# Layer 1 of a four-layer graph network: the later neighbours' numbers of blocks 4 to 7 made at step 12 instead of step 4, and in another PSUM bank

## The chip, the cores and the metric

The kernel runs on one core of a Trainium2 chip. A core has five engines that run side by side, each through its own list of instructions and in order: TensorE (PE; its weight loads are listed as PEld), VectorE (DVE), ScalarE (ACT), GpSimd (POOL) and SyncE (SP), which only starts transfers. They wait for one another by semaphores. TensorE writes into PSUM, which has eight banks of 512 float32 columns on each of 128 partitions; VectorE and ScalarE read it from there.

The metric is the time of one execution on the device, in microseconds (us). 0.2% of it is 1.15 us.

## The reference

Four layers pass over one graph of 4096 nodes with 64 features and an adjacency matrix of 4096 x 4096 zeros and ones (about four neighbours in a row). Each layer takes `h = max(layernorm(x), 0)` and adds something to `x`. Layer 0 is an attention with masked sigmoid scores, layers 2 and 3 are plain sums over neighbours. The change lies in layer 1:

```python
support = input @ weight
mask = (adj != 0).astype(support.dtype)
rank = jnp.cumsum(mask, axis=1)
deg = rank[:, -1:]
k = jnp.minimum(deg, float(MAX_NEIGH))          # MAX_NEIGH = 100
pos = rank - (deg - k)
w = mask * jnp.where(pos > 0, DECAY ** (k - pos), 0.0)   # DECAY = 0.5
out = w @ support + bias
```

A neighbour's weight is thus 0.5 to the power of the number of neighbours of the same row that come after it.

## The kernel before

**Tiles.** The adjacency matrix is kept transposed in on-chip memory as zeros and ones in fp8, in eight tiles `mask0` to `mask7`. A tile, or block `ib`, holds 512 rows of the matrix (`IB`); in it lie 32 chunks `t` of 128 neighbours each (`NT`), a chunk on 128 partitions. Blocks 0 to 3 are quad 0, blocks 4 to 7 quad 1.

**How a weight is made.** For a chunk, one matmul (`cnt`, L1500 in `counted`) counts for every neighbour the later ones, scaled so that the result, written as a 16-bit integer, is the bit pattern of 0.5 to that power in bf16. The constant matrix `after` counts the later ones inside the chunk. The number of neighbours in later chunks must be known beforehand; it is brought in through the last two partitions of the chunk, 126 and 127 (`KEPT`, `LANES`), where such numbers stand in the place of the mask's own rows. These two rows of the mask were copied aside earlier into `apart_m` (`taken`), are handled as a 33rd unit of their block (`t = -1`), and are put back afterwards (`given_back`, L1453).

**The numbers.** `chunks_counted(quad)` counts the neighbours of every chunk of a quad into a PSUM bank and copies the counts to `many`. `numbered(quad)` sums them over the later chunks: one matmul with `beyond` and four small ones with `pair` into a bank `pn`. VectorE then writes two fp8 rows `two`, the number capped at 120 and what is left of it, and copies started on SyncE's queue put them into partitions 126 and 127 of the quad's four masks, eight copies for quad 1. `numbered(0)` runs while the chunks of quad 1 are counted. `numbered(1)` runs inside the loop of layer 1.

**The loop of layer 1.** The blocks are taken in pairs (`GROUPS`: 0 and 1, 2 and 3, 4 and 5, 6 and 7). A pair has 66 units, its chunks from the last to the first and then the two rows set apart, and a step `k` (counted from 1) takes four of them: four `cnt` matmuls; four weights `w`, each a pass from PSUM to a 16-bit tile on ScalarE or VectorE; and the four products (`acc`, L1535) of the step before. So the pair 0, 1 takes steps 1 to 17, and quad 1 is first read at the beginning of the third pair, at 375.31 us of the profile. After the counts of each step, `step()` lets other work go on by one piece: the end of layer 0 for the last rows (`rows0`), the degrees (`degrees_of`), the rows of a finished pair (`rows1`). Then `check(2)` may run: VectorE checks that a piece of the adjacency matrix, read again from memory in float32 (`ckw`, 512 KB, three buffers, loads on SyncE's queue at L438), holds zeros and ones. A check first issues the next load, which waits until its buffer is read, and then checks the oldest one.

**The order** is written out by hand (`manual_schedule`); each engine runs its instructions as the program names them. Which engine makes a `w` is decided when the program is built: `Planned` sums what each engine was given, and VectorE takes a `w` where ScalarE would be late by the plan. All VectorE and ScalarE instructions go through a helper and are shown at L73.

**Banks.** The counts go round five banks, `COUNTS = (0, 1, 2, 5, 6)`, by a running index `turns[0]`; a step needs four of them. Two more banks hold the sums of the pair's blocks. The eighth, tag `pr` of pool `pm`, is the one in which rows are turned: `degrees_of` (`pd`), `rows0`, and from the second pair on `rows1` (`pr`, L1322) use it. Before the change `pn` takes the next of the five counting banks for both quads.

**SyncE's queue** carries, in the program's order: the loads for the checks, the copies of `two`, the two copies of `features_apart` (`apart_s`, L1485: the features that belong to the rows set apart, issued once the last rows of layer 0 are split on VectorE into `s2a`, read at step 17's products), and the copies of `given_back`.

Of the kernel before, what the change touches and what calls it, by code (L numbers as in the profile page):

```python
# [11 lines left out]
F32 = mybir.dt.float32  # L12
# [14 lines left out]
P = 128  # L27
NT = N // P
IB = 512
# [49 lines left out]
def kernel(  # L79
# [87 lines left out]
    def model(general):  # L167

        sfx = "_g" if general else ""
# [5 lines left out]
        def pool(name, bufs, on=stack, **kw):  # L175
            return on.enter_context(tc.tile_pool(name=name + sfx, bufs=bufs, **kw))
# [49 lines left out]
        pm = pool("pm", 1, space=PSUM)  # L226
# [143 lines left out]
        def push(job, lag):  # L370

            jobs.append([job, lag])
# [37 lines left out]
        def lane_of(ib, n):  # L410

            return masks[ib][KEPT + n : KEPT + n + 1, :, :]
# [780 lines left out]
        with tc.manual_schedule():  # L1193
# [20 lines left out]
            k, done = NG + 2, NG  # L1214
# [58 lines left out]
        def bank(b, name, shape=(P, IB)):  # L1273
            on = first_bank if b == COUNTS[-1] else banks
            return on.tile(list(shape), F32, tag=f"bank{b}", name=name + sfx)


        COUNTS = (0, 1, 2, 5, 6)
# [169 lines left out]
        many, turns = {}, [0]  # L1448
# [5 lines left out]

        def numbered(quad):

            pn = bank(COUNTS[turns[0] % len(COUNTS)], f"pn_{quad}")
            turns[0] += 1
            nc.tensor.matmul(
                pn, beyond, many[quad], start=True, stop=False, skip_group_check=True  # L1460
            )
            for q in range(QUAD):
                nc.tensor.matmul(
                    pn[q * NT : (q + 1) * NT, :], pair[:, quad, :], apart_m[:, q, :],
                    start=False, stop=q == QUAD - 1, skip_group_check=True,
                )
            two = temps.tile([P, LANES, IB], FP8, tag="two", name=f"two_{quad}{sfx}")
            dve.tensor_scalar(two[:, 0, :], pn, MOST, None, ALU.min, saturate=False)
            dve.scalar_tensor_tensor(
                two[:, 1, :], pn, MOST, two[:, 0, :], ALU.min, ALU.subtract,  # L1470
                saturate=False,
            )
            for q in range(QUAD):
                rows = slice(q * NT, (q + 1) * NT)
                for n in range(LANES):
                    queue = nc.scalar if n and quad == 0 and q < 2 else nc.sync
                    queue.dma_start(
                        out=lane_of(quad * QUAD + q, n).bitcast(F32),
                        in_=two[rows, n, :].bitcast(F32),
                    )  # L1480
# [9 lines left out]
        def counted(units):  # L1490


            cnts = []
            for ib, t in units:
                cnt = bank(COUNTS[turns[0] % len(COUNTS)], f"cnt_{ib}_{t}")
                turns[0] += 1
                by, what = after, masks[ib][:, max(t, 0), :]
                if t < 0:
                    by, what = apart[:, ib // QUAD, :], apart_m[:, ib % QUAD, :]
                nc.tensor.matmul(cnt, by, what, start=True, stop=True, skip_group_check=True)  # L1500
                cnts.append(cnt)
            for cnt, (ib, t) in zip(cnts, units):
                if t < 0:
                    lanes = slice(ib % QUAD * NT, (ib % QUAD + 1) * NT)
                    nc.tensor.matmul(
                        cnt, later[lanes, :], many[ib // QUAD][lanes, :],
                        start=False, stop=True, skip_group_check=True,
                    )
            return cnts
# [17 lines left out]
        with tc.manual_schedule():  # L1527
# [45 lines left out]
            late, k, moved, due = None, 0, False, 0.0  # L1573
            steps = NIB * (NT + 1) / CI
            clock[0] = max(dve.end, act.end)
            for blocks in GROUPS:
                units = [(ib, t) for t in reversed(range(-1, NT)) for ib in blocks]
                for at in range(0, len(units), CI):
                    these = units[at : at + CI]
                    cnts = counted(these)  # L1580
                    ws = weights(these, cnts)
                    if late is not None:
                        products(*late)
                    late = these, ws
                    k += 1
                    step()
                    due += CHECKS_1 / steps
                    free = clock[0] + ROUND + CHECK_LATE - dve.end
                    if due >= 1 and (free > dve.cost(CG * IB) or due >= 4):
                        check(2)  # L1590
                        due -= 1
                    clock[0] += ROUND
                    if k == 4 and not general:
                        numbered(1)
                    if not moved and len(ready.get(1, ())) == NIB:
                        features_apart()
                        moved = True
                assert moved
                if not general:
                    push(giving(blocks), 2)  # L1600
# [260 lines left out]
    with tc.If(any_odd[0] > 0):  # L1861
        model(True)
# [49 lines left out]
```

## Time and profile before

| | us |
|---|---|
| time, median of 3 runs | 573.25 (572.57 to 573.76) |
| the profiled execution | 572.18 |
| its span, first to last instruction | 569.5 |
| mean granted TensorE clock | 0.997 of full speed |
| layer 1's first pair: counts of step 1 / 6 / 12 / 17 start at | 311.62 / 322.05 / 332.42 / 341.05 |
| first counts of pair 2 / of pair 3 | 342.77 / 375.31 |

Times within the execution are counted from the first instruction. TensorE is busy 4.00 of the 4.00 us from 326 to 330, VectorE 2.77, ScalarE 3.70, GpSimd 3.11; in these stretches the transfers' share of the 16 DMA engines goes from 0.09 (322 to 326) to 0.91 (330 to 334). A line of the timeline gives the start, the duration, engine, line, operation, output and input, and in brackets the engine's idle time before it with what ended it. A merged line ("x4") spans the matmuls that follow one another; matmuls overlap, so that the distance from one start to the next tells the pace. The waits view gives, for an instruction and what it waited for, the total, the number and the longest.

### The profile page before, as it was taken

The numbers are of one execution on the slowest core, as the hardware profiler recorded it, in microseconds if no ns is written. First come the engines' busy times: TensorE is split into PE (matmuls) and PEld (weight loads), VectorE is DVE, ScalarE is ACT, GpSimd is POOL, SyncE is SP. The second block draws the span as 40 slices with busy tenths as digits, with TensorE's granted clock in tenths as the row PEclk, the third lists the DMA queues.
The fourth block names the chain that finished last, engine by engine and source line by source line (L and its number), as shares of the span: only waits on it lengthen the run. The fifth ranks groups of instructions, "written<-read, shape, count | busy, mean of one in ns | idle before, by whom it ended". The sixth has DMA issues, their size and how long they took to land.

```text
span 569.5 us, 9915 instructions
## 1 busy us (share of the span) xinstructions
PE 552.0 (97%) x3368; PEld 280.8 (49%) x3368; DVE 467.5 (82%) x949; ACT 358.8 (63%) x663; POOL 272.2 (48%) x526
## 2 busy tenths in 40 slices
PE   8999999999999999999999999999999999999995
PEld 3563333333333333333334444445454788888884
DVE  4679657799999999898976877778969897799993
ACT  3677667766676776778741888988888432342231
POOL 7624402675757576754444510384634343334332
PEclk9999999999999999999999999999999999999998
DMA  8995952689999999994223465453544788859960
GB/s 145 133 106 47 100 50 20 57 131 154 150 169 150 166 126 173 152 158 121 74 89 113 151 209 168 132 170 112 155 145 132 241 266 304 274 190 323 343 251 21
DMA packets 45612, 87.86 MB, mean 154 GB/s; under 512 B 6272, under 2 KB 24576, under 8 KB 45552
## 3 DMA queue, kind: packets, MB, share of 16 engines
q1 hardware_dynamic: 26112, 69.14, 36.5%
q0 software_dynamic: 18912, 17.77, 33.0%
q8 instruction: 28, 0.46, 0.3%
q10 hardware_dynamic: 528, 0.23, 0.2%
q14 instruction: 32, 0.26, 0.2%
HBM read 135.60 MB, written 1.05 MB: 240 GB/s over the span
## 4 chain that ended last, share of the span: by engine, by line
PE 70%; DVE 13%; POOL 5%; ACT 5%; issue 3%; DMA 2%; DVEq 0%; ACTq 0%; POOLq 0%; SPq 0%
PE acc L1090 15%; PE acc L1632 15%; PE ps L1059 15%; PE acc L1535 8%; PE cnt L1500 8%; PE idle L1183 3%; DVE att L73 3%; DVE ckw L73 2%; PE many L1387 1%; DMA s2a<-adjt_dram 1%; DVE s2a L73 1%; ACT ps L73 1%; DVE rrq L73 1%; POOL mask L211 1%; PE pt L266 1%
## 5 line engine op out<-in xcount | busy, mean ns | idle before, releaser
L1059 PE MATMUL ps<-qt,kt 64*128 64x512 f32 x512 | 123.4, 610 | 3.4 <-DVE att L73 3.0
L1090 PE MATMUL acc<-att,fb 128*64 128x512 f32 x512 | 117.8, 599 | 0.6 <-DVE att L73 0.5
L1632 PE MATMUL acc<-s,mask 128*128 128x256 f16 x1024 | 114.0, 273 | 0.4 <-DVE s L73 0.4
L73 ACT ACTIVATE w<-cnt 128x512 int16<-128x512 f32 x187 | 98.6, 606 | 12.1 <-PE cnt L1500 11.0
L1632 PEld LDWEIGHTS <-mask 128*128 128x128 fp8e4 x1024 | 99.8, 98 | 13.0 <-issue 1.0
L73 DVE TENSOR_TENSOR att<-ps,mask 128x1024 f32<-128x1024 f32 x82 | 98.6, 1217 | 8.6 <-ACT ps L73 8.5
L73 DVE SCALAR_TENSOR_TENSOR ckw<-ckw 128x1024 f32<-128x1024 f32 x76 | 96.0, 1274 | 4.2 <-DMA ckw<-adjt_dram 4.2
L73 ACT ACTIVATE ps<-ps,att_c,att_a 128x1024 f32<-128x1024 f32 x82 | 93.8, 1175 | 1.3 <-PE ps L1059 0.8
L73 ACT ACTIVATE att<-ps,att_c,att_a 128x1024 f32<-128x1024 f32 x46 | 54.6, 1202 | 54.1 <-PE ps L1059 53.9
L1059 PEld LDWEIGHTS ps<-qt,kt 64*128 64x128 f32 x512 | 44.8, 186 | 79.0 <-issue 28.7
L211 POOL DMA_DIRECT2D mask<-adjt_dram x128 | 70.1, 560 | 19.1 <-DMA mask<-adjt_dram 17.4
L73 DVE TENSOR_TENSOR att<-att,mask 128x1024 f32<-128x1024 f32 x46 | 56.9, 1252 | 18.8 <-ACT att L73 18.5
L1500 PE MATMUL cnt<-mask,after 128*128 128x512 fp8e4 x256 | 67.4, 379 | 2.7 <-DVE two L73 0.8
L1090 PEld LDWEIGHTS acc<-att,fb 128*64 128x64 f32 x512 | 33.5, 136 | 73.0 <-issue 67.6
L1535 PE MATMUL acc<-w,s2a 128*128 128x512 bf16 x256 | 66.2, 379 | 1.2 <-ACT asb L73 1.2
L73 DVE TENSOR_SCALAR w<-cnt 128x512 int16<-128x512 f32 x69 | 46.9, 686 | 22.6 <-PE cnt L1500 22.2
L301 POOL TENSOR_TENSOR rs_a<-rs_y 128x4 f32<-128x4 f32 x48 | 19.1, 398 | 67.4 <-DVE rs_y L73 61.0
L73 DVE SCALAR_TENSOR_TENSOR ck<-ck 128x512 f32<-128x512 f32 x60 | 42.8, 713 | 0.0
L1535 PEld LDWEIGHTS <-s2a 128*128 128x128 f16 x256 | 24.6, 98 | 33.6 <-issue 5.6
L1500 PEld LDWEIGHTS <-after 128*128 128x128 bf16 x256 | 24.4, 99 | 31.0 <-issue 2.7
L73 ACT ACTIVATE xm<-xm,inn 128x64 f32<-128x64 f32 x32 | 10.4, 347 | 45.9 <-DVE high L73 44.2
L1183 PE MATMUL idle<-ones 128*128 128x512 bf16 x126 | 30.9, 401 | 1.6 <-DVE ones L73 1.6
(248 smaller groups left out, 611.9 us busy)
## 6 DMA issues: line engine op xcount, KB each, us to landing
ckw<-adjt_dram SPq DMA_DIRECT2D x76, 512.0 KB, 4.3
mask<-adjt_dram POOLq DMA_DIRECT2D x128, 128.0 KB, 8.7
ck<-adjt_dram SPq DMA_DIRECT2D x60, 256.0 KB, 5.9
s2a<-adjt_dram SPq DMA_DIRECT2D x22, 512.0 KB, 4.9
x_sb<-x_dram SPq DMA_DIRECT2D x4, 256.0 KB, 7.5
out_dram<-y POOLq DMA_DIRECT2D x15, 64.0 KB, 3.7
apart_m<-mask SPq DMA_DIRECT2D x16, 16.0 KB, 4.1
mask<-apart_m SPq DMA_DIRECT2D x16, 16.0 KB, 4.3
```

The costliest lines, as they stand in the source:

```text
L73: return op(out, *args, **kw)
L211: nc.gpsimd.dma_start(out=masks[ib][:, g * CG : (g + 1) * CG, :], in_=adjt[ib, g])
L266: nc.tensor.transpose(pt[:, c, :], part, ident)
L301: nc.gpsimd.tensor_tensor(a, y, y, ALU.mult)
L1059: nc.tensor.matmul(ps[:, c, :], kt[half, g, :], qts[ib][half, :], start=True, stop=True)
L1090: nc.tensor.matmul(acc[c * D : (c + 1) * D, :], lhs[:, t, :], rhs[:, c, :], start=(at == 0), stop=(at == NG - 1), skip_group_check=True,)
L1183: nc.tensor.matmul(v.idle[:, v.filling % CG, :], ones, ones.unsqueeze(1).to_broadcast([P, IB // P, P]), start=True, stop=True, skip_group_ ...
L1387: nc.tensor.matmul(pc[q * NT : (q + 1) * NT, :], lane[:, NT - 1 - t : 2 * NT - 1 - t], masks[quad * QUAD + q][:, t, :], start=(t == 0), st ...
L1500: nc.tensor.matmul(cnt, by, what, start=True, stop=True, skip_group_check=True)
L1535: nc.tensor.matmul(accs[ib], apart_s if t < 0 else both(s2a, t), w, start=(t == NT - 1), stop=False, skip_group_check=True,)
L1632: nc.tensor.matmul(acc[:, to, :, :].rearrange("p k d -> p (k d)"), masks[ib][:, t, c * P : (c + 1) * P], s23[:, t, :, :].rearrange("p k d ...
```

## The change

`numbered(1)` is called at step 12 instead of step 4. Its `pn` comes from the bank in which rows are turned and doesn't take a turn of the five counting banks, so all counts after it go one bank back in the round. `numbered(0)` is as before.

```diff
         def numbered(quad):
 
-            pn = bank(COUNTS[turns[0] % len(COUNTS)], f"pn_{quad}")
-            turns[0] += 1
+            if quad == 0:
+                pn = bank(COUNTS[turns[0] % len(COUNTS)], f"pn_{quad}")
+                turns[0] += 1
+            else:
+                pn = pm.tile([P, IB], F32, tag="pr", name=f"pn_{quad}{sfx}")
             nc.tensor.matmul(
                 pn, beyond, many[quad], start=True, stop=False, skip_group_check=True
             )
...
                     clock[0] += ROUND
-                    if k == 4 and not general:
+                    if k == 12 and not general:
                         numbered(1)
```

In the order of each engine's instructions the change does this, beside the renumbering of banks:

- TensorE: the five matmuls of `pn` go from ahead of the counts of step 5 to ahead of those of step 13. The counts of steps 5 and 6 no longer name VectorE's `two` among what they wait for.
- VectorE: the two instructions of `two` go from behind the check of step 4 to behind the check of step 12, ahead of the split of the last rows. By the plan the fourth `w` of step 5, which ScalarE made before, now stands on VectorE in the place of `two`, and the fourth `w` of step 13 goes to ScalarE.
- SyncE: eight copies of `two` were followed by four loads for checks and then the two copies of `apart_s`; now the four loads come first, then the eight copies, then `apart_s`, and then the next three loads.
- GpSimd: nothing.

## The prediction

> **What bounds the kernel now.** I read the first page, then the waits of TensorE from 300 to 480 us, then the three engines' timelines around the two places that the change touches, and last the time that single loads take.
>
> ```profile
> PE 552.0 (97%) x3368; PEld 280.8 (49%) x3368; DVE 467.5 (82%) x949; ACT 358.8 (63%) x663; POOL 272.2 (48%) x526
> PEclk9999999999999999999999999999999999999998
> ```
>
> ```profile
> PE acc L1535 <- ACT asb L73: 1.2, 6, 0.2
> PE cnt L1500 <- DVE two L73: 0.8, 1, 0.8
> PE cnt L1500 <- ACT w L73: 0.7, 2, 0.4
> ```
>
> TensorE is busy 97% of the span at full clock, and its work is the same before and after. So the change is worth what it does to TensorE's idle time, and in layer 1 that is a handful of waits below 1 us. One of them, 0.8 us behind `two`, is the one the change is about. From 481.78 us the chain of waits is TensorE's sums of the last layers without a break, so idle time saved or added in layer 1 should reach the end unless a wait between takes it back.
>
> TensorE around the old place (start, duration, what):
>
> ```profile
> 318.71 0.38 PE L1459 MATMUL pn<-many,beyond 128*128 128x512 bf16 x1
> 319.02 0.40 PE L1463 MATMUL pn<-apart_m,pair 128*32 128x512 fp8e4 x4
> 319.35 1.04 PE L1500 MATMUL cnt<-mask,after 128*128 128x512 fp8e4 x4
> 322.05 1.04 PE L1500 MATMUL cnt<-mask,after 128*128 128x512 fp8e4 x4 [0.80 <-DVE two L73]
> 323.78 1.03 PE L1500 MATMUL cnt<-mask,after 128*128 128x512 fp8e4 x4
> 325.51 1.03 PE L1500 MATMUL cnt<-mask,after 128*128 128x512 fp8e4 x4
> ```
>
> A step (four counts, four products) takes 325.51 - 323.78 = 1.73 us. From step 5 (319.35) to step 6 (322.05) it is 2.70: 0.97 us are lost (the row says 0.80, as ends of matmuls are modelled). The five matmuls of `pn` take 319.35 - 318.71 = 0.64.
>
> VectorE at the old place, and where its columns checks meet the end of the first group:
>
> ```profile
> 319.44 1.21 DVE L73 SCALAR_TENSOR_TENSOR ckw<-ckw 128x1024 f32<-128x1024 f32 x1
> 320.58 0.68 DVE L73 TENSOR_SCALAR two<-pn 128x512 fp8e4<-128x512 f32 x1
> 321.30 0.69 DVE L73 SCALAR_TENSOR_TENSOR two<-pn,two 128x512 fp8e4<-128x512 f32 x1
> 340.99 1.22 DVE L73 SCALAR_TENSOR_TENSOR ckw<-ckw 128x1024 f32<-128x1024 f32 x1
> 342.14 1.22 DVE L73 SCALAR_TENSOR_TENSOR ckw<-ckw 128x1024 f32<-128x1024 f32 x1
> 343.83 0.69 DVE L73 TENSOR_SCALAR w<-cnt 128x512 int16<-128x512 f32 x1 [0.47 <-PE cnt L1500]
> ```
>
> The bank of `pn` is held until 321.99 since `two` stands behind a check. Later two checks stand next to each other, and a `w` (step 18, fourth unit) behind them.
>
> SyncE's queue, and one load that left it at 337.50:
>
> ```profile
> 321.29 5.50 SPq L1477 DMA_DIRECT2D mask<-two  x8
> 326.84 5.38 SPq L438 DMA_DIRECT2D ckw<-adjt_dram  x4
> 336.27 1.18 SPq L1485 DMA_DIRECT2D apart_s<-s2a  x2
> 337.50 5.07 SPq L438 DMA_DIRECT2D ckw<-adjt_dram  x3
> ```
>
> ```profile
> ckw<-adjt_dram SPq DMA_DIRECT2D x1, 512.0 KB, 3.4
> ```
>
> Eight little copies hold SyncE for 5.5 us. The load issued at 337.50 is the one that the second of the two adjoining checks reads: it lands at 337.50 + 3.4 = 340.9, only 1.2 us ahead of its use at 342.14.
>
> **The change part by part.**
>
> *Removed at step 4.* The 0.64 us of `pn` leave the path before step 5, and so does the hold of a counting bank: 0.97 us. What stands next there? In the program's order VectorE now has one `w` (0.61 to the next start) in the place of `two` (321.90 - 320.58 = 1.32); ScalarE has three `w` instead of four. That `w` runs from 320.58 to 321.26; its product, last of step 5 and now 1.61 us earlier, is issued at 321.30 + 0.65 = 321.95. It fits. VectorE itself gains only 0.71 us on its old times while TensorE gains 1.61, so its margin shrinks by 0.9 until it has caught up: it waits for GpSimd's reciprocal root (4.29 us from 322.80 to 327.09, now 0.73 earlier), so `xc` at 326.4, a check, and the `w` of step 9 at 328.0 to 328.6. Step 10 now starts at 328.96 - 1.61 = 327.35; its products begin 0.86 later and the fourth 0.65 after that, 328.86. Margin 0.2 us; I take 0, at worst 0.3. Step 12 starts at 332.42 - 1.61 = 330.81.
>
> *Added at step 12.* `pn` again 0.64 on TensorE (332.54 to 333.18), in the bank in which rows are turned. No count waits for that bank: its last readers (`pd`, 322.63) are done, and the next to use it comes at 348.39. So steps 13 on run 1.61 - 0.64 = 0.97 us early. `two` stands in VectorE's queue behind the check of step 12: the `w` of that step ran at 333.48 and the check at 334.09, 1.67 us after the counts, hence now at 332.48; `two` at 333.63 and 334.35, done 335.04. Behind it waits the split of the last rows (0.41), whose product is wanted after 339 (step 16), and the `w` of step 14, whose counts are not done before 336.0 (335.87 - 0.97 + 1.06, as 333.48 stood to 332.42). Both are covered. ScalarE takes four `w` in step 13 instead of three: 333.65 + 4 x 0.52 = 335.7, so its next three begin 0.3 us late; the third count bank is then free at 337.24 against 337.29 wanted. 0 us, at worst 0.2. If VectorE had no such gap, 1.3 us would show.
>
> *Moved on SyncE.* The eight copies leave the front of four loads and stand behind them. The four loads go earlier, which helps nobody (VectorE waited for none of these). Behind the copies now stand the two copies of `apart_s` and the load of the second adjoining check, which both were issued when the split was done (SyncE waited for it, 336.27). `two` at 333.63 was 320.58 before, and the first copy followed its start by 0.71: 334.34. With 5.50 for the eight and 0.05: `apart_s` at 339.89, the load 1.23 later, 341.1 instead of 337.5. Bounds of the batch: eight of the shortest copies in the trace (0.50) 4.0 us; at the rate of the first batch (six in 4.91, 306.70 to 311.61) 6.5. I take 5.5, the same eight copies with the loads quiet.
>
> `apart_s` lands 1.9 after its second issue (340.49): 342.4, wanted by the weight load at 343.4 - 0.97 = 342.4. Even, at most 0.4 us, and in the shadow of what follows.
>
> The load: single loads with others close behind landed in 3.1 (296.0), 3.5 (311.66), 3.7 (326.84) and 3.4 us (337.50); the median of all 76 is 4.3. I take 3.5: 344.6. The check is wanted at 342.14 - 0.97 = 341.17, so **VectorE stands 3.4 us**. Behind it in its queue is the `w` of step 18: 344.6 + 1.15 + 0.69 = 346.4. Its product was issued at 346.02 + 2 x 0.215 = 346.45 and could now go at 345.48. TensorE waits there, in order, about 0.95 us. The two `w` of step 19 follow at 347.1 and 347.7, wanted at about 347.3 (bank) and 348.1: free. VectorE has idle stretches of 1.87 us at 348 to 350, so it catches up, and the next two loads (issued about 341.6 and 342.1, at 4.2 and 5.0 as in the group of 311.66) land before their checks.
>
> **Sum.** -1.61 + 0.64 + 0.95 + about 0 = about 0 (-0.05). On the span 569.5 that is 569.5; the profiled execution 572.18 lies 2.7 above its span and 1.07 below the median, 573.25. I predict **573.2 us**. The bounds: batch 4.0 and load 3.1 give a release at 344.5, no wait, -0.97; batch 6.5 and load 4.3 give 346.4 + 1.0 + 0.8 = 348.2, +1.8.
>
> Two pages bear on this. The Trainium skill, "DMA: Bandwidth & Descriptors", Issuing engines are not separate DMA queues, says that the time a sequencer needs to start a DMA is usually small beside the DMA itself. Here eight starts take 5.5 us against 2.1 to 2.4 for the landing of each, so the trace does not agree; by the rule the batch would block nothing and the sum would be -0.97. The same page, Anatomy of one DMA, fits a DMA (issued by GpSimd) as 2.0 us plus bytes over 436 GB/s, an estimate of 3.2 us for 512 KB; by it the sum would be -0.35.
>
> **The rivals.**
>
> *The gain stays whole* (0.22). The batch goes through faster (two of its gaps, 0.93 and 0.86 at 322.01 and 323.50, may be waits that are over by step 12) and the load lands in 3.1: to be free, the `w` must be done by 345.48, the load landed by 343.6, 1.0 us sooner than I have it. For it: the shortest issues are 0.50. Against: none of the two batches was that fast. Net -0.97: 572.3.
>
> *The check costs more than the bank did* (0.30), slower. Same place: if the batch goes at the rate of 306.70 (first copy alone 1.73 us) or the load takes the median 4.3, the release is up to 348.2 and the net up to +1.8: 575.0. It decides against me from a landing at 345.8 on (+1.15). For it: three loads are now released together, and the load stands behind ten copies. Against: nothing else uses the DMA engines then.
>
> *The stall at step 6 stays under another name* (0.04): the `w` that VectorE takes over is late, or GpSimd's root holds `xc` and the `w` of step 9 costs what `two` did. Then the steps keep their old times, batch and load come 0.97 later still, and the `w` of step 18 is done at 347.4 instead of 346.45: +0.95, 574.2. The two `w` have 0.7 and 0.2 us of room, so I give it little.
>
> **How the numbers follow.** Forecast (gain given back) 0.44, whole gain 0.22, costlier check 0.30, other name 0.04. About 0.2%, 1.15 us, is what a measurement of this kernel can tell from no change. Forecast: -0.6 to +0.7, mostly within (0.37; 0.03 faster, 0.04 slower by the scatter of runs, 572.57 to 573.76). Whole gain: 0.17%, on the edge: 0.12 faster, 0.10 same. Costlier check: 0.28 slower, 0.02 same. Other name: 0.02 same, 0.02 slower. Faster 0.15, same 0.51, slower 0.34. The forecast's own range is 572.6 to 574.0; with the other cases 571.9 to 575.0.
>
> **What would show it.** In the changed profile: no wait for `two`, step 5 to 6 of 1.73 us, `pn` at about 332.5 with no wait behind it; eight copies on SyncE at about 334.3 for 5.5 us; a VectorE wait of some 3.4 us for a `ckw` load near 341 to 345; a TensorE wait for a `w` of VectorE of about 0.9 near 345.5, the third group's first step about where it was. No such VectorE wait makes the whole gain right; a wait above 2 us on TensorE there, the costlier check. A new wait anywhere else above 0.5 us would prove me wrong.

## The result and the profile after

| | before | after |
|---|---|---|
| median, 14 runs each on one chip, us | 573.23 (571.73 to 574.15) | 574.95 (573.08 to 578.62) |
| profiled execution, us | 572.18 | 575.78 |
| its span, us | 569.5 | 574.0 |

The ratio is 1.0036, 95% interval 1.0021 to 1.0052: the changed kernel is 2.1 us slower (1.2 to 3.0). "About nothing", 573.2, was forecast. Two repeats of it gave 1.0051 and 1.0043.

TensorE's work is the same in the first page of the changed kernel, at the same clock:

```profile
PE 552.8 (96%) x3368; PEld 281.0 (49%) x3368; DVE 467.5 (81%) x949; ACT 358.2 (62%) x663; POOL 270.9 (47%) x526
PEclk9999999999999999999999999999999999999998
```

So idle time is what to look for. TensorE's waits of the changed kernel from 300 to 480 us (total, number, longest):

```profile
PE acc L1538 <- DVE w L73: 1.4, 1, 1.4
PE acc L1538 <- ACT asb L73: 1.2, 6, 0.2
PE cnt L1503 <- DMA mask<-two: 1.2, 1, 1.2
PE cnt L1503 <- ACT w L73: 0.7, 2, 0.4
```

The 0.8 us behind `two` is gone. A wait of 1.4 us for a `w` of VectorE has come. The 1.2 us behind the copies of `two` for quad 0 (0.41 in the profile of before) is no part of the change: in the 20 profiles of this study it lies anywhere from 0.4 to 1.6 us, with or without the change (1.44 in an unchanged layer 1, experiment `before_flag`). It lies ahead of everything changed. The first count behind it starts 314.17 - 312.42 = 1.75 us later than before (0.76 of that by this wait, the rest was there already), and later times of this profile are compared with those of before after a shift of 1.75.

The old place and the new one, in TensorE's timeline:

```profile
320.47 1.02 PE L1503 MATMUL cnt<-mask,after 128*128 128x512 fp8e4 x4
322.19 1.03 PE L1503 MATMUL cnt<-mask,after 128*128 128x512 fp8e4 x4
...
334.28 0.38 PE L1462 MATMUL pn<-many,beyond 128*128 128x512 bf16 x1
334.58 0.40 PE L1466 MATMUL pn<-apart_m,pair 128*32 128x512 fp8e4 x4
334.92 1.04 PE L1503 MATMUL cnt<-mask,after 128*128 128x512 fp8e4 x4
```

From step 5 to 6 it is now 1.72 us (2.70 before), and `pn` costs 0.64 at step 12. SyncE's queue of the changed kernel:

```profile
336.07 5.03 SPq L1480 DMA_DIRECT2D mask<-two  x8
341.20 1.17 SPq L1488 DMA_DIRECT2D apart_s<-s2a  x2
342.42 1.52 SPq L438 DMA_DIRECT2D ckw<-adjt_dram  x3
```

VectorE, where the second of the two adjoining checks stands:

```profile
335.36 0.69 DVE L73 TENSOR_SCALAR two<-pn 128x512 fp8e4<-128x512 f32 x1
...
341.78 1.22 DVE L73 SCALAR_TENSOR_TENSOR ckw<-ckw 128x1024 f32<-128x1024 f32 x1
342.92 0.08 DVE L73 DVE_READ_ACCUMULATOR ckw<-ckw 128x1 f32 x1
347.02 1.23 DVE L73 SCALAR_TENSOR_TENSOR ckw<-ckw 128x1024 f32<-128x1024 f32 x1 [4.02 <-DMA ckw<-adjt_dram]
348.17 0.08 DVE L73 DVE_READ_ACCUMULATOR ckw<-ckw 128x1 f32 x1
348.17 1.88 DVE L73 TENSOR_SCALAR w<-cnt 128x512 int16<-128x512 f32 x3
```

And TensorE, where the products of step 17's weights run in order, and the fourth wants that `w`:

```profile
346.88 0.59 PE L1538 MATMUL acc<-w,s2a 128*128 128x512 bf16 x2 [0.20 <-ACT asb L73]
348.91 0.38 PE L1538 MATMUL acc<-w,s2a 128*128 128x512 bf16 x1 [1.44 <-DVE w L73]
349.12 1.02 PE L1503 MATMUL cnt<-mask,after 128*128 128x512 fp8e4 x4
```

Before, three of these products ran in one piece, the fourth among them:

```profile
346.02 0.81 PE L1535 MATMUL acc<-w,s2a 128*128 128x512 bf16 x3 [0.20 <-ACT asb L73]
```

The load left SyncE at 342.42 and landed 4.6 us later; VectorE stood 4.02 us; TensorE's fourth product, which could have gone at 346.88 + 0.43 = 347.31, waited.

**Where the time went.** All 20 profiles were cut at the same four rows: the count that waits for the copies of quad 0 (312.42 before), a count near the end of layer 1 (429.09), the first sum of layers 2 and 3 (478.57), the issue of the last output copy (565.04), and the end of the execution (its time, 572.18). The differences of these rows, in us:

| kernel | wait for `w`, step 18 | layer 1, 312.42 to 429.09 | layers 2 and 3, 478.57 to 565.04 | last copy to the end | 8 KB instruction packets in the last 8 us |
|---|---|---|---|---|---|
| before | none | 116.67 | 86.47 | 7.14 | 5 |
| after | 1.44 | 117.38 | 86.88 | 8.03 | 5 |
| `again` | 1.60 | 119.24 | 86.48 | 7.58 | 5 |
| `changed_3` | 0.88 | 116.82 | 86.62 | 7.91 | 5 |
| `hold_check` | none | 115.78 | 86.58 | 7.90 | 5 |
| `late_10` | 1.01 | 116.97 | 87.61 | 6.88 | 4 |
| `fetch_moved` | 0.56 | 116.43 | 86.48 | 6.40 | 4 |
| `before_shift` | none | 116.16 | 86.48 | 6.41 | 4 |

`again` and `changed_3` are the changed kernel. Its three profiles against the one of before: layer 1 +0.71, +2.57, +0.15 (mean +1.14); layers 2 and 3 +0.41, +0.01, +0.15 (+0.19); the end +0.89, +0.44, +0.77 (+0.70); the stretch from 429.09 to 478.57 +0.08. The sum is 2.11 us; 2.06 was measured over the runs. So the loss has a part in layer 1 and a part where nothing was changed, behind the last copy. The experiments took them apart.

That the sum comes so near is partly chance, for two reasons. One profile stands for the kernel before, and in the two others with its layer 1 that stretch takes 116.55 (`before_flag`) and 116.16 us (`before_shift`), since the wait behind `two` is 0.66 and 0.28 us there instead of 0.80:

```profile
322.99 1.04 PE L1500 MATMUL cnt<-mask,after 128*128 128x512 fp8e4 x4 [0.28 <-DVE two L73]
```

(`before_shift`; step 5 begins at 320.81, so 2.18 us from step 5 to 6.) What the change could win at step 6 thus ran from 0.45 to 0.97 us. And the last stretch is an execution's time less a row of its trace, while the recorded instructions stop earlier: time less span is 2.67 or 2.68 us in `before`, `before_flag` and `bank12`, and 1.69 to 1.83 in the 17 other profiles. Cut at the last recorded instruction, the end takes 4.46 us before and 6.25, 5.83 and 6.08 in the changed kernel. It is longer by either cut, but by how much depends on the cut.

### The profile page after: what moved, and what is told of

Read it like the earlier page. It is cut to its first block, busy times and chain, and to the rows that moved or that the text cites. A ratio compares the mean times of both kernels' runs of the same rounds, so it can differ in the third digit from the quotient of the medians.

```text
span 574.0 us, 9913 instructions
## 1 busy us (share of the span) xinstructions
PE 552.8 (96%) x3368; PEld 281.0 (49%) x3368; DVE 467.5 (81%) x949; ACT 358.2 (62%) x663; POOL 270.9 (47%) x526
## 4 chain that ended last, share of the span: by engine, by line
PE 53%; DVE 22%; DMA 8%; POOL 6%; issue 5%; ACT 4%; SPq 1%; ACTq 0%; DVEq 0%; POOLq 0%
PE acc L1090 13%; PE ps L1059 12%; PE cnt L1503 8%; PE acc L1538 8%; DVE ckw L73 6%; DVE att L73 4%; PE idle L1183 3%; DVE s2a L73 3%; DMA mask<-adjt_dram 3%; PE acc L1635 3%; DMA out_dram<-y 2%; PE many L1387 1%; DMA s2a<-adjt_dram 1%; POOL mask L211 1%; DVE y L73 1%
```

## The experiments

Each was timed beside the kernel before on its chip; a ratio is to that, with its 95% interval. Nothing is left out of the computation in any of them. "The changed kernel" is what the diffs start from unless another is named.

**The change again, and its three parts.** `again` is the changed kernel unedited.

> The changed kernel once more, for a second profile beside the first. Theory (the load behind eight copies on SyncE's queue): again a VectorE wait for a ckw load of 3.4 to 4.6 us near 343 to 347, a TensorE wait for a w of 1.2 to 1.8 us behind it, no wait for two; time +1 to +3 us against the kernel before. Rival (what is lost lies elsewhere: in the first profile 1.0 us were lost already by the first counts of layer 1, 0.8 at the wait for the copies of quad 0, and 1.9 after the last product): these three show again at about their size. If they don't, they are scatter, and the local balance of about +0.7 to +1.1 us is what the change costs.

575.25 us, 1.0051 [1.0031, 1.0072]. Its profile shows one thing more. TensorE at step 18:

```profile
345.16 0.59 PE L1538 MATMUL acc<-w,s2a 128*128 128x512 bf16 x2 [0.20 <-ACT asb L73]
347.35 0.59 PE L1538 MATMUL acc<-w,s2a 128*128 128x512 bf16 x1 [1.60 <-DVE w L73]
347.73 1.91 PE L1503 MATMUL cnt<-mask,after 128*128 128x512 fp8e4 x4
349.44 1.70 PE L1538 MATMUL acc<-w,s2a 128*128 128x512 bf16 x4
```

and TensorE's granted clock in stretches of 5 us (the column after the last bracket):

```profile
345.00:350.00 5.00, 3.24 (x9) 1.18 (x9) 4.49 (x8) 2.62 (x6) 0.00 (x0) 0.74 0.64 229
350.00:355.00 5.00, 5.00 (x27) 2.70 (x26) 2.50 (x6) 2.60 (x7) 0.00 (x0) 0.92 0.29 105
355.00:360.00 5.00, 5.00 (x29) 2.79 (x28) 3.40 (x8) 4.04 (x9) 0.83 (x2) 1.00 0.48 156
```

Four counts took 1.91 instead of 1.03 us. From the waiting product to the end of the next four products 350.97 - 347.35 = 3.62 us passed instead of 1.94: behind the wait of 1.60 the clock cost another 1.7. The profiles with waits of 1.44 and 0.88 keep the full clock there. So in this execution the wait was followed by a loss of its own size.

How often that happens can be estimated, as every run has its mean granted clock on record. It is 0.993 for this profile and 0.997 for the two others (even these fall short of 1 by their ends: 0.89 and 0.50 in the last two stretches of 3 us of the first). Of the 33 runs of the changed kernel 8 are at 0.994 or below, and they take 1.5 us more on the mean than the 25 others (576.7 against 575.1). Of 152 runs of the kernel before 2 are, and none of the 60 of `step8`, `step8_flag`, `hold_check`, `bank12_2` and `fetch_put_in`, whose ends are about as long and whose profiles show at most 0.4 us of wait at step 18. As an estimate, the clock costs the changed kernel 8 x 1.5 / 33 = 0.4 us a run.

`step8` calls `numbered(1)` at step 8, where the load for the adjoining check still gets through in time.

```diff
-                    if k == 12 and not general:
+                    if k == 8 and not general:
```

> Only the step is altered, 8 instead of 12; pn stays in the bank in which rows are turned. Theory: the eight copies are through about 7 us earlier, by about 334, ahead of the split of the last rows, so that apart_s and the load behind it leave as in the kernel before (336 to 338); no VectorE wait for that load, no TensorE wait for a w; the 0.97 us of step 5 stay won: about -1.0 us against the kernel before, 2 to 3 us under the changed kernel. Rival (the bank, or the new round of the counting banks, costs the time): as slow as the changed kernel, +1.5 to +2. Rival (more work for ScalarE at the step where two is made): within 0.3 us of the changed kernel.

573.06 us, 1.0005 [0.9993, 1.0017]. No wait for `w`; layer 1 takes 115.80 us, 0.87 less than before. But layers 2 and 3 take 87.55, 1.08 more, for this:

```profile
556.14 0.19 PE L1297 MATMUL pf<-one,bad 128*1 128x1 f32 x2 [1.01 <-DVE bad L73]
```

`pf`, the flag that says whether any check failed, stands in TensorE's list at a fixed place and waits for VectorE's last check, which comes when VectorE is through with all of them. A TensorE that arrives sooner waits there. The end, too, is longer than before's (7.76 against 7.14). So the -1.0 us expected is there in layer 1, and not in the time.

`pool_copies` starts the eight copies from GpSimd's queue, so that the load no longer stands behind them.

```diff
+                    if quad and not general:
+                        queue = nc.gpsimd
```

> Step 12 as in the changed kernel; the eight copies of two for quad 1 are started on GpSimd's queue instead of SyncE's. Theory (SyncE's order): apart_s leaves when the split is done and the load right behind it; no VectorE wait above 0.5 us at 341 to 347, no TensorE wait for a w there: about -1.0 us against the kernel before. Rival (the copies themselves, or the loads' contention, slow the load): the load still lands at 345 or later, and the time stays at +1 or more. Rival (the bank): no change from the changed kernel.

572.37 us, 0.9996 [0.9979, 1.0012]. The load leaves at 337.09, counted from the first of the four rows 4.1 us sooner than in the changed kernel (24.18 against 28.25 us), VectorE waits 1.08 us, TensorE not at all for a `w` there. The batch on SyncE is what made the load late. Layer 1 takes 115.82 us; of the -1.0 us expected in the time the medians show -0.7 and the ratio -0.2 (-1.2 to +0.7).

`double_copies` puts a second copy, into a tile that nobody reads, behind each of the eight.

```diff
+                    if more_copies is not None:
+                        half = slice(n * IB // 2, (n + 1) * IB // 2)
+                        nc.sync.dma_start(
+                            out=more_copies[rows, half].bitcast(F32),
+                            in_=two[rows, n, half].bitcast(F32),
+                        )
```

> The changed kernel with eight more small copies, each behind one of the eight, into a tile that nobody reads. Theory: the batch holds SyncE for about 10 instead of 5.0 us, the load leaves 4.5 to 5.5 us later, TensorE's waits near 344 to 354 (for apart_s and for the w) grow by the same amount to 6 to 7 us in all: +4.5 to +5.5 us against the changed kernel, about 580. Rival (the slowdown comes from elsewhere and the wait for the load is covered): under +1 us against the changed kernel.

578.97 us, 1.0115 [1.0095, 1.0135]. Sixteen issues hold SyncE from 336.19 to 346.2; `apart_s` and the load leave 5.0 us later than in the changed kernel, counted in the same way, and TensorE waits 4.22 us for `apart_s` and 0.37 for `w`. In the two stretches of 5 us from 345 to 355 the granted clock is 0.88 and 0.78. The expectation had 6 to 7 us of waits and about 580 us: the waits were shorter, and the fall of the clock may have made up for most of that.

`hold_check` makes no check at steps 17 and 18, so that the late one stands behind the `w` instead of ahead of it; all checks are made.

```diff
-                    if due >= 1 and (free > dve.cost(CG * IB) or due >= 4):
+                    if k not in (17, 18) and due >= 1 and (free > dve.cost(CG * IB) or due >= 4):
```

> The changed kernel, but no check of a ckw piece is made at steps 17 and 18; the check whose load is late then stands on VectorE behind the w of steps 18 and 19 instead of ahead of them. The copies stay on SyncE ahead of the load, which is as late as in the changed kernel. Theory (the late load costs only because a w stands behind its check in VectorE's queue): no TensorE wait for a w above 0.5 us at 343 to 350, the third group of steps begins about 2.4 us earlier than in the changed kernel, relative to step 6; time within 0.6 us of the kernel before, some 2 us under the changed kernel. Rival (TensorE waits for the copies or for the clock, whatever VectorE does): the wait stays, +1.5 to +2.

573.32 us, 1.0002 [0.9991, 1.0014]. TensorE's four products of step 18 run in one piece:

```profile
346.06 0.81 PE L1538 MATMUL acc<-w,s2a 128*128 128x512 bf16 x3 [0.20 <-ACT asb L73]
346.71 1.03 PE L1503 MATMUL cnt<-mask,after 128*128 128x512 fp8e4 x4
```

The load is as late as in the changed kernel (it leaves 28.25 us behind the first of the four rows in both, and lands in 4.7 us here), so what was taken away is only the check ahead of the `w`. Layer 1 takes 115.78 us, 2.03 less than the mean of the changed kernel's profiles, and the ratios differ by 1.9 to 2.8 us. Against the kernel before, 0.89 us are won in layer 1. They don't show in the time, as the end is 0.76 longer than before's.

`bank12` undoes the other half of the change: the numbers at step 12, but in a counting bank.

```diff
-            if quad == 0:
+            if True:
```

> Step 12 as in the changed kernel, but pn takes its turn among the five counting banks as before. Theory: a wait of TensorE for two of 0.5 to 1.0 us comes back at step 14, and the wait for the w of step 18 shrinks by the same, as its end is set by SyncE's queue; time within 0.5 us of the changed kernel, +1.3 to +2.5 against the kernel before. Rival (the bank in which rows are turned is what costs): 1 us or more faster than the changed kernel. Rival (waits add up): 0.8 to 1.0 us slower than the changed kernel.

573.35 us, 0.9995 [0.9982, 1.0009]. A miss: it was expected near the changed kernel, with a wait for `two` at step 14. There is no such wait: the later step alone removes it, whichever bank is used. Its load landed in 3.35 us rather than 4.6, the fourth product of step 18 waited only some 0.25 us, and its end is as short as before's (7.21). It differs from the changed kernel only in a bank, and yet in a load's landing: something else must move.

**Is the flag worth moving?** Three kernels make `pf` two flagged steps later.

```diff
-            steps = 7 if general else 4
+            steps = 7 if general else 6
```

> Step 8, and the matmul that sums the flags of the checks (pf) stands 16 sums of the last layers later in TensorE's order. Theory (at step 8 the 0.97 us of layer 1 are won, and 1.0 us is lost again at the end, where TensorE waits for the last check on VectorE): no wait for bad, -0.7 to -1.1 us against the kernel before. Rival (the gain is lost between, or the matmuls' work grew): same as step 8 alone, 0 to +0.3.

> The eight copies on GpSimd's queue at step 12, and pf 16 sums later. Theory as for step 8: no wait for bad, nor for the late load: -0.7 to -1.1 us against the kernel before, and about 0.3 to 0.8 under the kernel with the copies on GpSimd's queue alone. Rival (no wait takes the gain back at the end): within 0.2 us of that kernel.

> The kernel before with the sums of the last flag made two flagged steps later (6 instead of 4), and nothing of the change. Tells how much of the 1.1 us by which the version with copies on GpSimd's queue and the later flag beats the kernel before belongs to the flag alone. In the kernel before TensorE does not wait for the last check's flag at all (none in its profile), so theory 'the flag only matters when TensorE arrives earlier': within 0.3 us of the kernel before. Rival 'the later flag is worth its 0.5 us anywhere': -0.4 to -0.8 us.

`step8_flag` 572.87, 0.9989 [0.9976, 1.0003]; `pool_flag` 572.08, 0.998 [0.9966, 0.9994]; `before_flag` 573.01, 0.9986 [0.9966, 1.0005]. None of them waits for `bad` any more (86.47 to 86.48 us for layers 2 and 3). With the copies on GpSimd's queue the whole is faster than before. The edit alone can't be told from nothing, but its ratio (-0.8 us) is not within the 0.3 us expected either, so how much of the gain of `pool_flag` is the flag's stays open.

**What lengthens the load?** In the changed kernel's window from 345.2 to 346.2 us, inside the load, the queues read (packets, MB, share):

```profile
q1 hardware_dynamic: 93, 0.34, 93.2%
q14 instruction: 1, 0.01, 7.1%
```

A packet of the queue named "instruction" (8 KB: the profile's first page has 32 of them with 0.26 MB) took 1.1 us of one DMA engine (7.1% of 16 engine-microseconds) among the load's packets. In `bank12` it came at 345.0, just behind the load. To shift it, ScalarE's list was lengthened with one-column copies:

```diff
+            for _ in range(0 if general else 10):
+                nc.scalar.activation(tried, tried, AF.Copy)
             chunks_counted(0, {
```

> The changed kernel with ten one-column copies on ScalarE added ahead of the first neighbours' counts of layer 1, where ScalarE is idle for some 5 us (299.7 to 305.2 in the changed kernel's profile). Nothing else is changed; the added copies only move ScalarE's place in its instruction list, so that the 8 KB instruction fetch that fell inside the load of the later numbers (at about 345.2 in the changed kernel, load from 342.42 to 347.02, 4.6 us) should come about ten ScalarE instructions, some 4 to 5 us, earlier and so before the load is issued. Theory 'the fetch lengthens the load': the load lands in 3.3 to 3.6 us, VectorE waits about 2.7 to 3.0 us for it instead of 4.0, TensorE waits at most 0.5 us for w at step 18 instead of 1.4, and the time is within 0.6 us of the kernel before (-0.5 to +0.6). Rival 'three loads released together simply take 4.6 us': load 4.6, TensorE waits 1.3 to 1.6 us, +1.2 to +2.5 us.

> The changed kernel as it is, beside the two others on the same chip: both theories expect +1.2 to +3.0 us, a load of 4.6 to 4.7 us with the instruction fetch inside it, and TensorE waiting 1.4 to 1.6 us for w at step 18.

The copies depend on nothing, and the scheduler put them at 22.7 to 28.8 us of the execution, not where the program and the expectation have them; there they hide under other work. `fetch_moved`: 572.86 us, 0.9982 [0.9962, 1.0001]; `changed_3` on the same chip 575.48, 1.0043 [1.0020, 1.0066]. With ten tiny instructions more, the whole loss is gone. In `fetch_moved` the packet comes at 337.5, the load lands in 3.65 us (4.04 in `changed_3`), and the wait for `w` is 0.56 us:

```profile
347.35 0.38 PE L1538 MATMUL acc<-w,s2a 128*128 128x512 bf16 x1 [0.56 <-DVE w L73]
```

So load and wait came out near the theory's bounds (3.6 and 0.5 us), but they are the smaller part of the time: against `changed_3` layer 1 gains 0.39 us, and the stretch behind the last copy 1.5.

The other direction was tried twice, with four and then two such copies in `bank12`, and `early_4` is the changed kernel with four.

> The version with the numbers at step 12 but in the bank of the counting round (1.000 of the kernel before, its load landed in 3.3 us), with four one-column copies on ScalarE added at the same place ahead of the first neighbours' counts. Its ScalarE fetch stood at about 345.0 us, just behind a load from 341.56 to 344.86; four instructions earlier it should stand at about 343 and so inside the load. Theory 'the fetch lengthens the load': the load lands in 4.4 to 4.8 us, TensorE waits 1.0 to 1.5 us for w at step 18, and the time becomes that of the changed kernel, +1.2 to +2.5 us. Rival 'the bank is what makes the difference' (the turning bank hands the late check a worse moment): load 3.3 to 3.6, TensorE waits at most 0.4 us, within 0.5 us of the kernel before.

> The numbers at step 12 in the counting round's bank, with two such copies early. Four of them moved ScalarE's fetch from 345.0 to 340.5 us, ahead of the load; two should put it at about 343, inside the load issued at about 341.6. Theory 'the fetch lengthens the load': load 4.0 to 4.7 us and TensorE waits 0.9 to 1.6 us for w at step 18, the time +0.8 to +2.0 us. Rival 'the bank makes the difference': load 3.3 to 3.6 us and at most 0.4 us of wait, within 0.5 us of the kernel before.

> The changed kernel with four such copies early instead of ten. In the ten-copy version ScalarE's fetch moved from about 344.5 to 337.5 us; four copies moved it by about 4.5 us in the other version, so it should stand at about 340, just before the load's issue at about 342. Theory 'the fetch lengthens the load': load 3.3 to 3.7 us, TensorE waits at most 0.6 us, and the time is 0.3 to 1.2 us below the changed kernel's +2 us by this alone, more or less by what the end of the program does. Rival: load 4.0 to 4.7 and wait 0.9 to 1.6.

`fetch_put_in` 573.99, 1.0007 [0.9987, 1.0027]: the packet went to 340.5, ahead of the load, which landed in 3.55; its end grew to 8.45 us, the longest of all. `bank12_2` 573.13, 1.0002 [0.9986, 1.0017]: the packet came at 344.6, inside the load (341.67 to 345.10), and the load landed in 3.43 all the same: against the theory. `early_4` 572.47, 0.9986 [0.9971, 1.0001]: packet at 340, load 3.43, wait 0.34, end 6.54 us; in its profiled execution TensorE waits 2.43 us for `bad`, but this execution is the slowest of its twelve (573.81).

**Layer 1 or the end?** `late_shift` was to lengthen ScalarE's list behind step 18 only, and `before_shift` lengthens it in the kernel before, at the place of `fetch_moved`.

```diff
+                for _ in range(10):
+                    nc.scalar.activation(tried, tried, AF.Copy)
                 both_summed()
```

> The changed kernel with ten one-column copies on ScalarE added only ahead of layers 2 and 3 (ScalarE is busy 7.9 of 22 us there), so that everything to step 18 is as in the changed kernel and only the end of ScalarE's list is shifted as in the version with ten early copies. Theory 'the load at step 18 costs it': the load still lands in 4.0 to 4.7 us, TensorE waits 0.9 to 1.6 us for w, and the time stays +1.2 to +2.5 us over the kernel before. Rival 'the end of the program costs it': from the last output copy's issue to the end 6.4 us rather than 7.9, and the time comes down to within 0.8 us of the kernel before (0 to +0.8) although step 18 still waits.

> The kernel before with ten one-column copies on ScalarE added ahead of the first neighbours' counts, as in fetch_moved. No wait for w at step 18 is there to be shortened. Theory 'only the load at step 18 matters': within 0.4 us of the kernel before. Rival 'where the lists end matters by itself': the time moves by 0.7 to 1.5 us either way, with the stretch behind the last output copy's issue (7.1 us in the kernel before's profile) changed by as much.

`late_shift` 572.30, 0.9988 [0.9975, 1.0001]. It does not separate anything: the scheduler moved these ten to 23 us as well, packet (338.0), load (3.54) and end (6.05) with them. It is in effect `fetch_moved` once more, and agrees with it. `before_shift` 572.59, 0.9991 [0.9976, 1.0007]: its profile has an end of 6.41 us instead of 7.14 (to the last recorded instruction 4.65 instead of 4.46); the time can't be told from no change.

`late_10` binds the ten copies to a tile made in layers 2 and 3; they run at 492.97.

```diff
+            for _ in range(10 if tag == 2 else 0):
+                nc.scalar.activation(tried, h[:, 0, 0:1], AF.Copy)
```

> The changed kernel with ten one-column copies on ScalarE that read a tile made early in layers 2 and 3 (about 495 us), so that ScalarE's list is the changed kernel's up to there and shifted by ten behind it. The load at step 18 should land in 4.0 to 4.7 us with the fetch inside it and TensorE wait 0.9 to 1.6 us for w, as in the changed kernel. Theory 'both cost, about half each': 6.0 to 6.5 us from the last output copy's issue to the end instead of 7.6 to 8.0, and +0.3 to +1.2 us over the kernel before. Rival 'the load at step 18 alone': +1.5 to +2.5 us. Rival 'the end alone': -0.5 to +0.2 us.

573.32 us, 1.0000 [0.9982, 1.0017]. Step 18 is the changed kernel's: the load lands in 4.17 us and TensorE waits.

```profile
347.36 0.38 PE L1538 MATMUL acc<-w,s2a 128*128 128x512 bf16 x1 [1.01 <-DVE w L73]
```

The end is 6.88 us. By the medians this is the "both" of the expectation (+0.3), by the ratio (0.0, from -1.0 to +1.0) the rival "the end alone"; it does not part them. Layer 1 is as slow as in `changed_3` (116.97 against 116.82), and yet some 2 us less were measured than for the changed kernel. From the first row to the end the profiles have 260.31 us, against 261.61, 262.80 and 261.21 for the changed kernel and 259.76 before; 1.0 of the difference to `changed_3` lies in the end, and a wait of 1.07 for `bad` takes as much back. A part of what remains may be the clock's: all 12 runs have a mean of 0.996 or more. What the end is made of, in the queues' view of the 8 us from the last copy's issue (packets, MB, share), for the changed kernel

```profile
q10 hardware_dynamic: 144, 0.03, 2.1%
q14 instruction: 5, 0.04, 1.6%
q8 instruction: 1, 0.02, 0.8%
```

and for `late_10`:

```profile
q10 hardware_dynamic: 144, 0.03, 2.1%
q14 instruction: 4, 0.03, 1.6%
q8 instruction: 1, 0.02, 1.1%
```

One packet fewer. In the 20 profiles the twelve with five packets have an end of 7.1 to 8.45 us, the eight with four 6.05 to 6.9, without an overlap. Cut at the last recorded instruction there is one: `before`, `before_flag` and `bank12` with five packets have 4.40 to 4.54 us, the nine others with five 5.83 to 6.69, the eight with four 4.29 to 5.20.

**The fastest version** has the copies on GpSimd's queue, the flag two flagged steps later and the ten copies.

> The version with the eight copies on GpSimd's queue and the later flag (-1.1 us, no wait for w at step 18, 6.7 us behind the last output copy's issue), with ten copies early in ScalarE's list. Theory 'the end's length adds by itself': 6.0 to 6.4 us behind the last output copy's issue and -1.3 to -1.8 us against the kernel before. Rival 'the shift only helps by the load at step 18': -0.8 to -1.2 us, as without it.

571.84 us, 0.9973 [0.9956, 0.9991]: 1.5 us below the kernel before (0.5 to 2.5), so it beats both kernels. Layer 1 takes 115.73 us, the flag waits for nothing, the end takes 6.89 with four packets. `pool_flag` without the ten copies also had four (6.71), so the shift had nothing to add there: the time is where the theory put it (-1.3 to -1.8), but not for its reason, an end of 6.0 to 6.4 us.

## Why the prediction was wrong

In short: the path was right, and three sizes on it were not. The load was taken at 3.5 us and landed in 4.0 to 4.8, which makes +0.15 and +0.71 us in layer 1 where -0.05 was forecast. And two terms were put at nothing without a reason: the granted clock, some 0.4 us a run, and the stretch behind the last copy, 0.70 us. Layer 1 at full clock stayed within the forecast's own range (-0.6 to +0.7) or on its edge; these two terms took the time out of it.

Times of the prediction are shifted by the 1.75 us named above.

1. *Step 6 loses its wait, 0.97 us; `pn` costs 0.64 at either place.* Right: 1.72 us from step 5 to 6, 0.64 at step 12, no wait for its bank. But 0.97 is the largest of three profiles with the old order; the two others have 0.82 and 0.45.
2. *What stands behind `two` on VectorE and ScalarE is covered.* Right: `two` at 335.36 (335.38 forecast), the split at 336.69, the `w` of step 14 waited for its counts.
3. *Eight copies from 334.34 for 5.5 us.* Started at 336.07 (336.09 forecast), took 5.03. The bounds held, though one row was misread: of the first batch it is the fifth copy (309.25) that takes 1.73 us, the first takes 0.55. The Trainium skill, "DMA: Bandwidth & Descriptors", Issuing engines are not separate DMA queues, says that a start is usually small beside the DMA itself. One start took 0.50 to 0.59 us here and one copy 2.1 to 2.5 to land: the page fits one start, and eight in a row are not small. `pool_copies` shows what the batch costs the load, 4.1 us.
4. *The load lands in 3.5 us, VectorE stands 3.4, TensorE waits 0.95.* Here a term was mis-sized. The load left 0.43 us sooner than forecast and landed in 4.6, 4.8 and 4.0 us in the three profiles of the changed kernel; 3.5 was the row of a load that nothing else met. "Nothing else uses the DMA engines then" did not hold: the two loads behind it left within 1.2 us, and an instruction packet fell among them. TensorE's wait was 1.44, 1.60 and 0.88. In the first profile the fourth product came at 348.91, forecast 346.43 + 1.75 = 348.18: 0.73 late, so that the wait cost 0.95 + 0.73 = 1.68 us, which makes -0.97 + 1.68 = +0.71 for layer 1.
5. *The granted clock stays.* Not said, but in the sum: one of three profiles pays another 1.7 us behind its wait, and 8 of 33 runs have a mean clock as low as that one's or nearly.
6. *Time saved or lost in layer 1 reaches the end unless a wait between takes it back.* True of losses. Of the gain of `step8` 1.1 us are taken back at `bad`. The prediction read the waits between 300 and 480 us and the chain behind 481.78, not what stands ready to become a wait behind it.
7. *Nothing happens behind the last copy.* Not said either, as the sum was made on the span with a fixed 2.7 us around it. These 2.7 are 1.8 in the changed kernel, while the recorded instructions behind the last copy take 1.4 to 1.8 us longer; together it loses 0.70 us there on the mean of its profiles, and no case of the prediction had it. Where it comes from is not known.

So the mechanism was the forecast's and the rival's alike (a check that a late load holds up, shown by `hold_check` and `pool_copies`), and its size in layer 1, +0.15 and +0.71 in the two profiles with the full clock, lies between them: the load landed at 347.02, where the rival was to decide from 345.8 + 1.75 = 347.55 on. That the time came out on the rival's side (+1.8) is partly luck for the rival: the clock and the end carried it there, and the rival had neither. The two rivals without a costlier wait fell: a wait for `w` there is, and step 6 keeps no wait under another name.

**What stays open.** That an instruction packet inside a load lengthens it is likely, not settled. With the numbers at step 12, loads without one landed in 3.35 to 3.65 us (`bank12`, `fetch_moved`, `late_shift`, `early_4`, `fetch_put_in`, `double_copies`), with one in 4.0 to 4.8 (the three of the changed kernel, `late_10`, `hold_check`). But with one inside, `bank12_2` has 3.43 and `before_shift`, in the old order, 3.3, and a longer load also has more time to meet a packet (in `bank12` it came 0.1 us behind the landing). Other things lengthen a load too: 3.8 and 3.9 us without a packet in `step8` and `step8_flag`, and 5.0 to 5.7, with a packet, beside the copies on GpSimd's queue. That three loads leave together is not enough: they do so in seven kernels with 3.35 to 3.65. Four or five packets part the ends if these are cut at the execution's time, not if they are cut at the last recorded instruction; so what makes the changed kernel's end longer than before's, with five packets in both, no run tells. Where the clock fell in the seven other runs with a low mean isn't on record, as only one execution in each series is profiled.

## What to carry to other kernels

A batch of small DMA starts is a block of time on its queue, and moving it moves every load behind it: look for the load with the least room, and for what stands behind its reader. A load's landing is worth taking with the worst of its rows when its reader stands in an engine's list ahead of something on the critical path; here it was cheaper to put the `w` ahead of the column check, or to start the copies elsewhere, than to hope for 3.5 us. When two kernels differ by 0.3%, compare the stretches before and behind the changed place too, and the mean clock of all runs: a loss may lie in the program's end or in a part of the executions. A control that only lengthens one engine's instruction list can show how much of a difference has nothing to do with the change.

## What the runs showed of the hardware

- A wait of 1.60 us was followed by 3.6 us at about half the granted clock (0.74 and 0.92 in stretches of 5 us); around one of 4.22 it was 0.88 and 0.78; after 1.44 and 0.88 us it stayed at 1.00. The Trainium skill, "TensorE: Matmul & The Clock Gate", HAM oscillation, gives the rule to have no idle gap beyond about 3.4 us; here a fall of the clock followed a gap of less than half of that.
- Ten one-column ScalarE copies, 0.2 us each where ScalarE had room, went with a difference of 2.6 us (575.48 to 572.86). With them an instruction packet moved from 344.5 to 337.5 us, and one of five was gone from the last 8 us; that they act through the packets is likely and not shown. The Trainium skill, "Runtime: NRT & Kernel Launch", Instruction fetch mechanics, says that crossing from one block of instructions to the next is mostly hidden, but that a taken branch to a block not at hand stalls until it is fetched. The program ends with a branch over its general path, and four or five packets are fetched in the last 8 us; whether an engine waited for one of them the trace doesn't show.
